# Moving a gate product and a normalisation between engines in a row LSTM, with a new written order

## The chip, the cores and the metric

The kernel runs on one core of one Trainium2 chip. The metric is the device time of a whole execution in microseconds (us). Five engines matter: TensorE (PE, with its weight loads listed apart as PEld), VectorE (DVE), ScalarE (ACT), GpSimd (POOL), and SyncE (SP), which only issues DMAs. Each engine works through its own queue in order, and waits on semaphores that other engines raise.

## The reference, cut to what matters

An image batch of shape (8, 96, 128, 128) is normalised in 32 groups of channels, and then a row LSTM runs down the 128 rows. A row needs the hidden row above it, so rows cannot run side by side.

```python
x_n = gn(x)                                  # (g - mean) / sqrt(var + eps), 32 groups
its = conv(x_n, W_is * mask)                 # width 3, 96 -> 384 channels; the mask leaves
                                             # the left and (by thirds) the centre tap
def step(h, c, row):                         # once for each of 128 rows
    gates = conv(h, W_ss) + row              # width 3, 96 -> 384 channels
    f, i, o = sigmoid(three quarters); g = tanh(the fourth)
    c = f * c + i * g
    h = o * tanh(c)
out = x + h of every row
```

All data are 32-bit floats.

## The kernel before, in words

The batch is cut into two halves of four images (`s` = 0 and 1). A **half-step** `n = 2*row + s` computes one row of one half; there are 256, and the two halves take turns, so that one half's gates are worked on while the other half's products run. Before the first half-step, all of x is read once for the group statistics (some 140 us); that part is not touched.

The pixels of a row are held as even and odd pixels (64 each), and the width-3 convolution is done with fewer products: of the hidden row `hx` the kernel forms a sum `vs` (`total`, letter S), a difference `vf` (`difference`, F), both on VectorE, and two shifted differences `vd` (`shifted`, D), on GpSimd. Of x's 64 "own" channels the like is formed ahead of time into `xs` (letters P, Q, E below); x's 32 "shared" channels are normalised into partitions 96 to 127 of `hx` and ride along with the hidden row.

The 384 gate channels are three PSUM banks A, B, C per half-step, each 128 partitions (sorted so that bank A holds all of f, B all of i, C all of o in partitions 0 to 95, and each a third of g in partitions 96 to 127) by 512 columns (even half, odd half). Every product is 64 rows deep and 256 columns wide; TensorE holds two such products side by side, one in rows 0 to 63 and one in rows 64 to 127 ("lanes" below), and each product is two passes in the trace (two LDWEIGHTS, two MATMULs). A half-step has 33 products: `1`, `2`, `0`, `3` twice for each bank (they use `vs`, `vf`, and both halves of `vd`), and `P`, `Q`, `E` once for each bank. The order between them is:

- `1`, `2`, `P`, `Q` into the bank, then `cp` (`copy`, ScalarE) copies the even half with the bias into an SBUF tile `m`, then `lo` and `hi` (`even`, `odd`, VectorE) replace the two halves by sum and difference, then `0`, `3`, `E` are accumulated on top.
- `si` and `ta` (`sigmoid`, `tanh`, ScalarE) make the gates, `fg` is f*c, `gt` (`gated`) i*g, `ce` (`cell`) the sum, `th` its tanh, `ou` (`output`) o*tanh(c), written into the next row of `hx`. `re` (`residual`) adds h to x in place, on GpSimd, and the result is stored.
- `W` calls `prepare`, the work for the next block of four rows: for one image of the half, `widen` (normalise the own channels), the sum and the two differences into `xs` (all GpSimd), `normalise_shared` for the shared channels (GpSimd), and at times `load_rows` (a DMA).

The scheduler is switched off for PE, ScalarE, VectorE and GpSimd (`manual_schedule`): instructions stand in each engine's queue in the order of the string `PERIOD`, which `do(n, PERIOD)` walks once per half-step. A mark shifts a name to another half-step: `'` is n-1, `''` is n-2, `+` is n+1 (for S, F, D two are added). So one walk of the string holds the products of half-step n, the gates of n-1, and the residual of n-2. A trailing `a` or `b` means the even or the odd pixels alone.

One explicit dependency matters below: `shifted` on GpSimd waits until VectorE has done the last of S and F (`self.last`).

Of the kernel before, what the change touches and what calls it, by code (L numbers as in the profile page):

```python
# [21 lines left out]
def kernel(  # L22
# [35 lines left out]
    NH = 2  # L58
# [232 lines left out]
    def norm(engine, dst, src, lo, layout, b):  # L291
        s, j = divmod(b, BH)
        scale, shift = rstd[s][lo:P, layout, j : j + 1], nmr[s][lo:P, layout, j : j + 1]
        if engine is nc.scalar:
            return engine.activation(dst, src, AF.Identity, bias=shift, scale=scale)  # L295
        else:
            return engine.tensor_scalar(dst, src, scale, shift, ALU.mult, ALU.add)  # L297
# [11 lines left out]
            s * BH + j,  # L309
        )  # L310

    def combine(xw, n, total, differences):

        e, o = xw[:, 0:n, 0:J], xw[:, 0:n, J + 1 :]
        nc.gpsimd.tensor_add(total, e, o)  # L315
        nc.gpsimd.tensor_sub(  # L316
            differences,
            strided(xw[:, 0, :], 0, [(W + 1, n), (J, 2), (1, J)]),
            strided(xw[:, 0, :], J + 1, [(W + 1, n), (0, 2), (1, J)]),
        )  # L320

    def own_image(s, k, j):

# [11 lines left out]
            to[:, r, 1:3, lo:hi].rearrange("p t b j -> p b t j"),  # L335
        )

    normalised = {}

    def normalise_shared(engine, s, k, j, lo, hi):  # L340

        normalised[s, k] = norm(
            engine,
            strided(
                hx[s][k % 2][C:P, lo, 0, j, :],
                0,
                [(2 * BH * JP, hi - lo), (BH * JP + 1, 2), (1, J)],
            ),
            (x0[C:P, 1, j : j + 1] if s == 1 and k == lo == 0 else xt[s, k][C:P, j, lo:hi, :])
            .rearrange("p r (j t) -> p r t j", t=2),  # L350
            C,
            0,
            s * BH + j,
        )
# [53 lines left out]
    class HalfStep:  # L408


        def __init__(self, n):
            self.n, (self.row, self.s) = n, divmod(n, NH)
            self.ps, self.m1, self.moving, self.done, self.gates, self.th = {}, {}, {}, set(), None, None
            self.started, self.images, self.halves, self.writer = set(), {}, {}, {}
            self.hx = hx[self.s][self.row // R % 2][:, self.row % R]
            self.xs = xs[self.s][self.row // R % 2][:, self.row % R]
            self.c = cs[self.s].rearrange("p t b j -> p (t b j)")
# [102 lines left out]
            nc.scalar.activation(self.part(g, lo, hi, t), self.part(ps, lo, hi, t), AF.Tanh)  # L520


        def sigmoid(self, a):
            if self.row == 0 and a == 0:
                return
            gate = self.ps[a][0:C]
            nc.scalar.activation(gate, gate, AF.Sigmoid)  # L527

        def forget(self):
            f = self.ps[0][0:C]  # L530
# [3 lines left out]
        def gated(self, lo=0, hi=BH, t=None):  # L534
            to = self.g if self.row > 0 else self.c
            to, i, g = (self.part(ap, lo, hi, t) for ap in (to, self.ps[1][0:C], self.g))
            nc.vector.tensor_mul(to, i, g)  # L537


        def part(self, ap, lo, hi, t=None):  # L540
            ap = ap.rearrange("p (t b j) -> p t b j", t=2, b=BH)
            return ap[:, :, lo:hi] if t is None else ap[:, t, lo:hi]
# [28 lines left out]
        def total(self, engine=nc.vector, lo=0, hi=BH):  # L571
            e, o = self.pair(lo, hi)
            self.last = engine.tensor_add(self.operand("vs")[:, 0, lo:hi], e, o)  # L573
            row, s = divmod(self.n + 1, NH)
            if engine is nc.vector and row >= R and row % R < 2 and (s, row // R) in normalised:
                tc.add_manual_dep(
                    self.last.ins,
                    normalised[s, row // R].ins.name,
                    mybir.DependencyInfo(mybir.DependencyClass.Sync, mybir.DependencyReason.DATA),
                    reason="the next difference finds the next rows of x normalised",  # L580
                )

        def difference(self, engine=nc.vector, lo=0, hi=BH):
            e, o = self.pair(lo, hi)
# [2 lines left out]
        def shifted(self, lo=0, hi=BH):  # L587
            h = self.hx[:, 0, lo, :]
            diff = nc.gpsimd.tensor_sub(  # L589
                self.operand("vd", 2)[:, :, lo:hi],  # L590
                strided(h, 1, [(BH * JP - 1, 2), (JP, hi - lo), (1, J)]),
                strided(h, 0, [(BH * JP + 1, 2), (JP, hi - lo), (1, J)]),
            )
            if self.last.ins.engine != E.Pool:
                tc.add_manual_dep(
                    diff.ins,
                    self.last.ins.name,
                    mybir.DependencyInfo(
                        mybir.DependencyClass.Sync, mybir.DependencyReason.SCHED_ONLY
                    ),  # L600
                    reason="GpSimd starts when VectorE is done with both SBUF reads",
                )

        def residual(self):
            s, row = self.s, self.row
            xo = xt[s, row // R][0:C, :, row % R, :].rearrange("p b (j t) -> p t b j", t=2)
            (nc.gpsimd if 2 * row + s < last else nc.vector).tensor_add(xo, xo, self.h)  # L607

    def store(s, k, lo, hi):
        nc.sync.dma_start(  # L610
# [6 lines left out]

    SHARED = (((0, 0, R), (3, 0, 1)), ((1, 0, R),), ((2, 0, R),), ((3, 1, R),))

    def own(s, *images):  # L620
        return [(own_image, s, 1, j) for j in images]

    def shared(s, k, *images):
        return [
            (normalise_shared, nc.gpsimd, s, k, *(j if isinstance(j, tuple) else (j, 0, R)))
            for j in images
        ]

    FIRST = [
        own(0, 0),  # L630
        own(0, 1),
        own(0, 2) + shared(0, 1, 0, 1),
        own(0, 3) + [(load_rows, 0, 2)] + shared(0, 1, 2, 3),
        own(1, 0, 1),
        own(1, 2) + shared(1, 1, 0, 1),
        own(1, 3) + [(load_rows, 1, 2)] + shared(1, 1, 2, 3),
        [(own_image, 0, 2, 0), (own_image, 1, 2, 0)],
    ]

    def work(n):  # L640
        if n < len(FIRST):
            return FIRST[n]
        row, s = divmod(n, NH)
        k, r = divmod(row, R)
        parts = []
        if r == R - 1 and k + 2 < NB:
            parts.append((own_image, s, k + 2, 0))
        elif r < R - 1 and k + 1 < NB:
            parts.append((own_image, s, k + 1, r + 1))
        if k + 1 < NB:  # L650
            parts += shared(s, k + 1, *SHARED[r])
        if r == R - 2 and k + 2 < NB:
            parts.append((load_rows, s, k + 2))
        return parts

    worked = set()

    def prepare(n):
        if n not in worked:
            worked.add(n)  # L660
            for part, *args in work(n):
                part(*args)

    def finish(n):
        prepare(n)
# [10 lines left out]


    PERIOD = (
        "2A hiC' siA' D'' 1B 1A taA' 2B fg' 3C' 1A 0C' re'' taB' 2A 2B EC' 1B cpA 0C' 2C W loA cpB "
        "3C' 1C siB' loB PB+ QA+ hiA taCb' 2C hiB taCa' 0A gtb' 1C siC' gta' EA 0B ceb' cpC 3A PA+ "  # L680
        "cea' thb' PC+ 3B loC tha' QC+ oub' EB oua' QB+ 3A F' 3B 0A S' 0B"
    )
    PIXELS = {"a": (0, BH, 0), "b": (0, BH, 1)}
    SPLIT = ("taC", "gt", "ce", "th", "ou")
    PARTS = {
# [12 lines left out]
    def do(n, names, by_lanes=False):  # L698

        for name in names.split():  # L700
            if name == "W":
                prepare(n - 1)
                continue
            at = n
            for mark, offset in (("'", -1), ("+", 1), ("*", 2)):
                at += offset * name.count(mark)
                name = name.replace(mark, "")
            pixels = PIXELS[name[-1]] if name[:-1] in SPLIT and name[-1] in PIXELS else ()
            whole_name = name[:-1] if pixels else name
            tile_ = whole_name[-1] if whole_name[-1] in order else ""  # L710
            part = whole_name[: len(whole_name) - len(tile_)]

            if part in ("S", "F", "D"):
                at += NH
            if not 0 <= at <= last:
                continue
            step = half_step(at)
            if name in step.done or whole_name in step.done:
                continue
            if by_lanes and (part in OWN or part in H_PRODUCTS) and (  # L720
                at < last or part in ("P", "Q") or (part, order[tile_]) in step.halves
            ):
                if step.piece(part, order[tile_]):
                    step.done.add(name)
                continue
            step.done.add(name)
            getattr(step, PARTS[part])(*([order[tile_]] if tile_ else []), *pixels)
            if by_lanes and part == "re":
                finish(at)
# [273 lines left out]
```

## Time and profile before

| what | us |
| --- | --- |
| three runs | 2023.32, 2023.80, 2024.15 (median 2023.8) |
| the profiled execution | 2027.04, its span 2025.2 |
| 153 to 2018 us of the span | the row LSTM; from about 205 us on, one half-step every 7.33 us |
| time before that | statistics of x, and the first rows |
| granted TensorE clock | 0.997 |

The profile is one execution. Its times are taken from its own span; the three unprofiled runs lie about 3 us below it, and a forecast made against the span is moved by the same difference to the median. An instruction's duration and the distance between the starts of two neighbours on an engine are not the same: a short activation's neighbour starts before it has ended, a long one's only after. Where a sum below needs the second, it is read from starts in the timeline.

A few groups (by line, with shapes kept apart) that the later text does not show again:

| group | count | mean us |
| --- | --- | --- |
| GpSimd, own channels: widen 128x512 / sum 128x256 / differences 128x512 | 252 each | 0.816 / 0.641 / 1.070 |
| GpSimd, shared channels 32x512, 32x384, 32x128 | 188, 64, 60 | 0.816, 0.696, 0.464 |
| GpSimd, shifted differences / residual | 255 | 1.041 / 1.297 |
| VectorE, gate product 96x256 | 506 | 0.412 |

### The profile page before, as it was taken

Reading aid. Unit: us, or ns where it says so; the run is one execution under the profiler, and the core shown is the slowest. Engines: PE = TensorE matmul, PEld = TensorE weight load, DVE = VectorE, ACT = ScalarE, POOL = GpSimd, SP = SyncE. Lnnn points to the kernel's source line nnn. Section 1 sums busy time; section 2 is a strip of 40 time slices with the busy share of each in tenths; the row PEclk is TensorE's granted clock in tenths of the full one; section 3 lists DMA queues with packets and bytes.
Section 4 is the critical chain, followed back from the end, with each engine's and each line's share of the span. In section 5 each row is a group of like instructions: output and inputs, shape, how many; then the busy total and the mean of one; then the engine's idle time right before and its main releaser. Section 6 shows DMA issues by size and latency. Waiting matters only on the chain.

```text
span 2025.2 us, 44842 instructions
## 1 busy us (share of the span) xinstructions
PE 1923.3 (95%) x16936; PEld 1831.0 (90%) x16936; DVE 1529.1 (76%) x3996; ACT 1494.9 (74%) x3161; POOL 1473.1 (73%) x1712
## 2 busy tenths in 40 slices
PE   0289999999999999999999999999999999999998
PEld 0178999999999999999999999999999999999997
DVE  5767777777777777777777777777777777777776
ACT  3776777777777777777777777777777777777776
POOL 3348777777777777777777777777777777777752
PEclk9989999999999999999999999999999999999999
DMA  9994333444334334433433443343344333434411
GB/s 374 424 310 100 98 103 91 112 115 104 82 89 113 92 101 115 113 83 82 110 95 95 116 116 95 79 100 96 93 116 116 96 82 96 107 92 106 116 33 32
DMA packets 103382, 237.11 MB, mean 117 GB/s; under 512 B 5952, under 2 KB 8896, under 8 KB 97280
## 3 DMA queue, kind: packets, MB, share of 16 engines
q1 hardware_dynamic: 103168, 234.25, 42.0%
q8 instruction: 135, 2.21, 0.5%
q14 instruction: 79, 0.65, 0.1%
HBM read 183.90 MB, written 50.33 MB: 116 GB/s over the span
## 4 chain that ended last, share of the span: by engine, by line
PE 93%; DMA 4%; ACT 2%; DVE 1%; issue 0%; SPq 0%; POOL 0%; DVEq 0%; POOLq 0%
PE ps L442 92%; DMA piece<-in_x_dram 3%; DMA xs<-in_x_dram 1%; ACT piece L216 1%; PE ps L174 0%; ACT piece L217 0%; DVE bst L876 0%; ACT hx L295 0%; ACT piece L295 0%; DVE hx L560 0%; ACT xs L216 0%; ACT xs L217 0%; SPq L864 0%; PE pv L251 0%; DVE ps L516 0%
## 5 line engine op out<-in xcount | busy, mean ns | idle before, releaser
L442 PE MATMUL ps<-vd,wl 64*128 64x256 f32 (+1 forms) x6096 | 1390.9, 379 | 0.3
L442 PEld LDWEIGHTS ps<-vd,wl 64*128 64x128 f32 (+1 forms) x6096 | 1028.4, 186 | 45.7 <-issue 2.4
L442 PE MATMUL ps<-vs,wm 64*128 64x256 f32 (+1 forms) x3052 | 775.1, 380 | 4.9 <-POOL vs L573 4.4
L442 PE MATMUL ps<-vf,wm 64*128 64x256 f32 (+1 forms) x3052 | 766.3, 377 | 0.0
L527 ACT ACTIVATE ps<-ps 96x512 f32<-96x512 f32 x766 | 441.6, 577 | 356.2 <-PE ps L442 348.1
L442 PE MATMUL ps<-xs,wx 64*128 64x256 f32 x3080 | 637.8, 377 | 11.1 <-POOL xs L315 11.1
L589 POOL TENSOR_TENSOR vd<-hx 128x512 f32<-128x512 f32 x257 | 266.7, 1038 | 388.5 <-PE ps L442 384.8
L442 PEld LDWEIGHTS ps<-xs,wx 64*128 64x128 f32 x3080 | 494.0, 187 | 14.2 <-POOL xs L315 11.6
L520 ACT ACTIVATE g<-ps 32x256 f32<-32x256 f32 (+1 forms) x1021 | 468.6, 482 | 26.7 <-PE ps L442 6.3
L442 PEld LDWEIGHTS ps<-vf,wm 64*128 64x128 f32 (+1 forms) x3052 | 475.4, 187 | 11.0 <-PE ps L442 0.4
L442 PEld LDWEIGHTS ps<-vs,wm 64*128 64x128 f32 (+1 forms) x3052 | 459.6, 186 | 21.6 <-POOL vs L573 5.4
L512 DVE TENSOR_TENSOR ps<-m,ps 128x256 f32<-128x256 f32 x768 | 326.0, 425 | 192.5 <-ACT m L508 182.0
L442 PE MATMUL ps<-xs,wt 64*128 64x256 f32 x1530 | 453.2, 377 | 0.6 <-DVE ps L516 0.6
L508 ACT ACTIVATE m<-ps,wl 128x256 f32<-128x256 f32 x766 | 361.6, 474 | 90.9 <-PE ps L442 84.3
L532 DVE TENSOR_TENSOR ps<-ps,c 96x512 f32<-96x512 f32 x254 | 176.8, 696 | 232.9 <-PE ps L442 226.9
L607 POOL TENSOR_TENSOR x<-x,hx 96x512 f32<-96x512 f32 x255 | 330.8, 1297 | 6.7 <-DVE hx L560 6.7
L516 DVE TENSOR_TENSOR ps<-m,ps 128x256 f32<-128x256 f32 x768 | 300.8, 422 | 1.3 <-PE ps L442 1.2
L442 PEld LDWEIGHTS ps<-xs,wt 64*128 64x128 f32 x1530 | 280.0, 186 | 12.8 <-DVE ps L516 1.0
L316 POOL TENSOR_TENSOR xs<-xw 128x512 f32<-128x512 f32 (+1 forms) x254 | 270.9, 1067 | 0.0
L297 POOL TENSOR_SCALAR hx<-x,rstd,nmr 32x384 f32<-32x384 f32 (+2 forms) x312 | 225.8, 724 | 33.2 <-DMA x<-in_x_dram 1.1
L297 POOL TENSOR_SCALAR xw<-xr,rstd,nmr 128x512 f32<-128x512 f32 x252 | 205.6, 816 | 7.1 <-DVE nmr L289 6.5
L537 DVE TENSOR_TENSOR g<-ps,g 96x256 f32<-96x256 f32 x507 | 189.0, 413 | 3.8 <-ACT g L520 3.8
(91 smaller groups left out, 1223.1 us busy)
## 6 DMA issues: line engine op xcount, KB each, us to landing
xr<-in_x_dram SPq DMA_DIRECT2D x124, 512.0 KB, 6.4
x<-in_x_dram SPq DMA_DIRECT2D x63, 768.0 KB, 6.1
out_dram<-x SPq DMA_DIRECT2D x62, 768.0 KB, 4.6
xs<-in_x_dram SPq DMA_DIRECT2D x30, 1024.0 KB, 12.3
piece<-in_x_dram SPq DMA_DIRECT2D x16, 1024.0 KB, 12.3
x<-in_x_dram SPq DMA_DIRECT2D x62, 256.0 KB, 3.2
xs<-in_x_dram SPq DMA_DIRECT2D x4, 512.0 KB, 8.7
out_dram<-x SPq DMA_DIRECT2D x2, 576.0 KB, 3.7
```

The costliest lines, as they stand in the source:

```text
L297: return engine.tensor_scalar(dst, src, scale, shift, ALU.mult, ALU.add)
L316: nc.gpsimd.tensor_sub(differences, strided(xw[:, 0, :], 0, [(W + 1, n), (J, 2), (1, J)]), strided(xw[:, 0, :], J + 1, [(W + 1, n), (0, 2) ...
L442: made = nc.tensor.matmul(self.ps[a][:, bass.ts(half, HB)][:, cols], weights[rows, bass.ts(a, P)], rhs[rows, cols], start=new, stop=False, ...
L508: nc.scalar.activation(self.m1[a], m1, AF.Identity, bias=column)
L512: nc.vector.tensor_add(self.ps[a][:, 0:HB], self.m1[a], self.ps[a][:, HB:])
L516: nc.vector.tensor_sub(hi, self.m1[a], hi)
L520: nc.scalar.activation(self.part(g, lo, hi, t), self.part(ps, lo, hi, t), AF.Tanh)
L527: nc.scalar.activation(gate, gate, AF.Sigmoid)
L532: nc.vector.tensor_mul(f, f, self.c)
L537: nc.vector.tensor_mul(to, i, g)
L589: diff = nc.gpsimd.tensor_sub(self.operand("vd", 2)[:, :, lo:hi], strided(h, 1, [(BH * JP - 1, 2), (JP, hi - lo), (1, J)]), strided(h, 0, ...
L607: (nc.gpsimd if 2 * row + s < last else nc.vector).tensor_add(xo, xo, self.h)
```

## The change

- The even pixels' part of i*g (`gta`) is done by GpSimd. [...]the sigmoid of bank B is split in two halves of 256 columns (`siBb` in place, `siBa` into a new SBUF tile `i`). From half-step 3 on this holds for all but the last.
- The shared channels are normalised on ScalarE (one image per half-step, 32x512 or 32x384), and the few 32x128 parts on VectorE; both are called `U` and stand for half-step n-2.
- The own channels' work is cut in three (`W1`, `W2`, `W3`: widen, sum, differences), which stand apart in the string; `load_rows` follows the last of them. The first block's work is laid out anew (`FIRST`, `LATER`): one image per half-step, with one image spread over three.
- S stands before F; products of `vs` stand before products of `vf`. The dependency of `total` on the GpSimd normalisation goes. `residual` is, like `shifted`, held until VectorE has done the last of S and F of its half.
- `PERIOD` is rewritten: among others `siA` moves from the start of the next walk to the end of its own, `hiA` stands directly behind `loA`, `taA'` stands between `cpA` and `cpB`, `P+` of banks B and C come first, and `gtb'` stands before `hiB`.

```diff
-    def combine(xw, n, total, differences):
-        e, o = xw[:, 0:n, 0:J], xw[:, 0:n, J + 1 :]
-        nc.gpsimd.tensor_add(total, e, o)
+    def add_pixels(xw, n, total):
+        nc.gpsimd.tensor_add(total, xw[:, 0:n, 0:J], xw[:, 0:n, J + 1 :])
+    def subtract_pixels(xw, n, differences):
         nc.gpsimd.tensor_sub(
...
-        def sigmoid(self, a):
+        def sigmoid(self, a, lo=0, hi=BH, t=None):
             if self.row == 0 and a == 0:
                 return
-            gate = self.ps[a][0:C]
-            nc.scalar.activation(gate, gate, AF.Sigmoid)
+            gate = self.part(self.ps[a][0:C], lo, hi, t)
+            if t == 0 and self.n > NH:
+                self.even_input = self.tile("i", (C, HB))
+                to = self.even_input.rearrange("p (b j) -> p b j", b=BH)
+            else:
+                to = gate
+            nc.scalar.activation(to, gate, AF.Sigmoid)
...
-            nc.vector.tensor_mul(to, i, g)
+            if t == 0 and self.even_input is not None:
+                i = self.even_input.rearrange("p (b j) -> p b j", b=BH)
+                nc.gpsimd.tensor_mul(to, i, g)
+            else:
+                nc.vector.tensor_mul(to, i, g)
...
-            row, s = divmod(self.n + 1, NH)
-            if engine is nc.vector and row >= R and row % R < 2 and (s, row // R) in normalised:
-                tc.add_manual_dep(
...
-            (nc.gpsimd if 2 * row + s < last else nc.vector).tensor_add(xo, xo, self.h)
+            made = (nc.gpsimd if 2 * row + s < last else nc.vector).tensor_add(xo, xo, self.h)
+            following = steps.get(self.n + NH)
+            if self.n < last and following is not None:
+                following.hold(made)
...
-    def own(s, *images):
-        return [(own_image, s, 1, j) for j in images]
+    def own(s, k, j, buffer=0):
+        to, wide = xs[s][k % 2], xw[buffer]
+        return (
+            (widen, nc.gpsimd, wide, 0, R, s, k, j, 0),
+            (add_pixels, wide, R, to[:, :, 0, j, :]),
+            (subtract_pixels, wide, R, to[:, :, 1:3, j, :]),
+        )
     def shared(s, k, *images):
+        parts = [j if isinstance(j, tuple) else (j, 0, R) for j in images]
         return [
-            (normalise_shared, nc.gpsimd, s, k, *(j if isinstance(j, tuple) else (j, 0, R)))
-            for j in images
+            (normalise_shared, nc.vector if hi == 1 else nc.scalar, s, k, j, lo, hi)
+            for j, lo, hi in parts
         ]
+    spread = own(1, 1, 0, 1)
     FIRST = [
-        own(0, 0),
-        own(0, 1),
-        own(0, 2) + shared(0, 1, 0, 1),
-        own(0, 3) + [(load_rows, 0, 2)] + shared(0, 1, 2, 3),
-        own(1, 0, 1),
-        own(1, 2) + shared(1, 1, 0, 1),
-        own(1, 3) + [(load_rows, 1, 2)] + shared(1, 1, 2, 3),
-        [(own_image, 0, 2, 0), (own_image, 1, 2, 0)],
+        ([], own(0, 1, 0), []),
+        (shared(0, 1, 0, 1), own(0, 1, 1), []),
+        (shared(0, 1, 2, 3), own(0, 1, 2), []),
+        (shared(1, 1, 0, 1), own(0, 1, 3), [spread[0], (load_rows, 0, 2)]),
+        (shared(1, 1, 2), own(1, 1, 1), [spread[1]]),
+        (shared(1, 1, 3), own(1, 1, 2), [spread[2]]),
+        ([], own(1, 1, 3), [(load_rows, 1, 2)]),
+        ([], own(0, 2, 0), []),
     ]
+    LATER = dict(zip((9, 11, 13), own(1, 2, 0, 1)))
...
     PERIOD = (
-        "2A hiC' siA' D'' 1B 1A taA' 2B fg' 3C' 1A 0C' re'' taB' 2A 2B EC' 1B cpA 0C' 2C W loA cpB "
-        "3C' 1C siB' loB PB+ QA+ hiA taCb' 2C hiB taCa' 0A gtb' 1C siC' gta' EA 0B ceb' cpC 3A PA+ "
-        "cea' thb' PC+ 3B loC tha' QC+ oub' EB oua' QB+ 3A F' 3B 0A S' 0B"
+        "1A hiC' D'' U 1B fg' 2A 2B siBb' 0C' 1A re'' taB' 3C' 2A 1B siBa' EC' 2B cpA 3C' W1 1C "
+        "taA' loA 0C' 2C cpB hiA PB+ PC+ W2 taCb' loB 2C taCa' 0A gtb' 1C gta' siC' 3A hiB PA+ "
+        "ceb' QB+ cpC W3 3B cea' EA thb' loC 0B tha' QC+ oub' 3A oua' EB 0A S' 0B QA+ F' siA 3B"
     )
-    SPLIT = ("taC", "gt", "ce", "th", "ou")
+    SPLIT = ("taC", "siB", "gt", "ce", "th", "ou")
...
-            if name == "W":
-                prepare(n - 1)
+            if name[0] == "U":
+                if n >= NH:
+                    prepare(n - NH, "U")
+                continue
+            if name[0] == "W":
+                prepare(n - 1 + name.count("+") - name.count("'"), name.strip("W+'"))
                 continue
```

More of the change, by code (lines that the diff above doesn't have):

```diff
@@ L320, in combine @@
         )
+    def combine(xw, n, total, differences):
+        add_pixels(xw, n, total)
+        subtract_pixels(xw, n, differences)
     def own_image(s, k, j):
@@ L336, in own_row @@
         )
-    normalised = {}
     def normalise_shared(engine, s, k, j, lo, hi):
-        normalised[s, k] = norm(
+        norm(
             engine,
@@ L414, in __init__ @@
             self.started, self.images, self.halves, self.writer = set(), {}, {}, {}
+            self.even_input = self.last = None
             self.hx = hx[self.s][self.row // R % 2][:, self.row % R]
@@ L573, in total @@
             self.last = engine.tensor_add(self.operand("vs")[:, 0, lo:hi], e, o)
-            row, s = divmod(self.n + 1, NH)
-            if engine is nc.vector and row >= R and row % R < 2 and (s, row // R) in normalised:
-                tc.add_manual_dep(
[L577 to L581, printed above, removed]
         def difference(self, engine=nc.vector, lo=0, hi=BH):
@@ L593, in shifted, with hold @@
             )
-            if self.last.ins.engine != E.Pool:
+            self.hold(diff)
+        def hold(self, made):
+            if self.last is not None and self.last.ins.engine != E.Pool:
                 tc.add_manual_dep(
-                    diff.ins,
+                    made.ins,
                     self.last.ins.name,
@@ L644, in work, with prepare @@
         k, r = divmod(row, R)
[L645 to L662, printed above, removed]
+        ahead, image = (k + 2, 0) if r == R - 1 else (k + 1, r + 1)
+        return (
+            shared(s, k + 1, *SHARED[r]) if k + 1 < NB else [],
+            own(s, ahead, image) if ahead < NB else (),
+            ([(load_rows, s, k + 2)] if r == R - 2 and k + 2 < NB else [])
+            + ([LATER[n]] if n in LATER else []),
+        )
+    worked = {}
+    def prepare(n, which="123"):
+        scalar, image, rest = worked.setdefault(n, [list(parts) for parts in work(n)])
+        now = []
+        if "U" in which:
+            now, scalar[:] = list(scalar), []
+        for i in "123":
+            if i in which and int(i) <= len(image) and image[int(i) - 1]:
+                now.append(image[int(i) - 1])
+                image[int(i) - 1] = None
+        if image.count(None) == len(image) and n not in closed:
+            closed.add(n)
+            now += rest
+        for part, *args in now:
+            part(*args)
+    closed = set()
     def finish(n):
```

## The prediction

> **What bounds the kernel now.** I read the page first, then the timeline of one half-step engine by engine, then the form-separated list for ScalarE. From the page, the busy line and the chain:
>
> ```profile
> PE 1923.3 (95%) x16936; PEld 1831.0 (90%) x16936; DVE 1529.1 (76%) x3996; ACT 1494.9 (74%) x3161; POOL 1473.1 (73%) x1712
> PE 93%; DMA 4%; ACT 2%; DVE 1%; issue 0%; SPq 0%; POOL 0%; DVEq 0%; POOLq 0%
> ```
>
> TensorE bounds it; the other three are a quarter idle. "Busy" does not say that both lanes run, though. The timeline of the weight loads shows one lane standing still once in each half-step:
>
> ```profile
> 1004.55 0.19 PEld L442 LDWEIGHTS ps<-vd,wl 64*128 64x128 f32 x1
> 1004.59 0.19 PEld L442 LDWEIGHTS ps<-vs,wm 64*128 64x128 f32 x1
> 1004.77 0.44 PEld L442 LDWEIGHTS ps<-xs,wx 64*128 64x128 f32 x4
> 1005.24 0.36 PEld L442 LDWEIGHTS ps<-vf,wm 64*128 64x128 f32 x2
> 1005.74 0.18 PEld L442 LDWEIGHTS ps<-vd,wl 64*128 64x128 f32 x1
> 1005.77 0.18 PEld L442 LDWEIGHTS ps<-vs,wm 64*128 64x128 f32 x1
> ```
>
> On each lane a pass follows the last after 0.216 us (1004.55 to 1004.77), so a product takes 0.433 and 33 of them on two lanes 33 x 0.433 / 2 = 7.13 us. From 1005.24 on only `2C` is loaded; `0A` (the `vd` load), due on the other lane at about 1005.2, comes at 1005.74. The timelines of VectorE and ScalarE tell what it waited for:
>
> ```profile
> 1004.39 0.90 DVE L512 TENSOR_TENSOR ps<-m,ps 128x256 f32<-128x256 f32 x2 [0.70 <-ACT m L508]
> 1005.20 0.76 DVE L516 TENSOR_TENSOR ps<-m,ps 128x256 f32<-128x256 f32 x2
> ...
> 1001.76 0.57 ACT L527 ACTIVATE ps<-ps 96x512 f32<-96x512 f32 x1 [1.38 <-PE ps L442]
> 1002.37 1.21 ACT L520 ACTIVATE g<-ps 32x512 f32<-32x512 f32 x2
> 1003.89 0.94 ACT L508 ACTIVATE m<-ps,wl 128x256 f32<-128x256 f32 x2 [0.31 <-PE ps L442]
> 1004.73 0.58 ACT L527 ACTIVATE ps<-ps 96x512 f32<-96x512 f32 x1
> 1005.33 0.65 ACT L520 ACTIVATE g<-ps 32x256 f32<-32x256 f32 x2
> 1006.01 0.57 ACT L527 ACTIVATE ps<-ps 96x512 f32<-96x512 f32 x1
> 1006.61 0.47 ACT L508 ACTIVATE m<-ps,wl 128x256 f32<-128x256 f32 x1
> 1006.99 0.73 ACT L552 ACTIVATE th<-c 96x256 f32<-96x256 f32 x2
> ```
>
> `hiA` (the first of the two at 1005.20, 0.42 long) ends at 1005.62 and `0A` loads 0.12 later. `hiA` stood behind `loB`, which waited for `cpB`, which waited for the second `1B`. That is a loop, and it gives the period: `1B` (two passes to its end, 0.59, and 0.04 to ScalarE) + `cpB` 0.475 + 0.03 + `loB` to `hiA` 0.335 + `hiA` 0.42 + 0.22 to `0A` at full cadence + 0.04 for the other lane behind it + 12 products on that lane to the next `1B`, 5.18 = 7.33. The timeline has `siA` at 1001.76 and again at 1009.10: 7.33 to 7.34. So 0.20 us of a half-step is lost, some 50 us in the whole run, and nothing else is to be had.
>
> **What the Trainium skill says.** "ScalarE: Activation LUTs", What ACT_TABLE_LOAD costs: an activation costs 186 ns plus 0.833 ns an element, 93 more for each pointer operand, and neighbours overlap by 93 ns. The trace agrees on durations (`th`, 256 wide: 0.411; 399 ns by the page) but on the overlap only for 256 columns: `cpC` to `th` is 0.38 for 0.47, yet behind 512 columns the next starts 0.02 after the end (1006.01 + 0.57, then 1006.61). "SBUF — State Buffer", Who interferes with whom: VectorE with two SBUF inputs contends with GpSimd reading SBUF. Only S and F have two; in the trace of before they run at 1000.97 to 1001.73, where GpSimd idles, so that cost isn't seen. "GPSIMD Engine Reference", 3.1 Elementwise, has GpSimd's tensor_tensor at about twice VectorE's time; here 0.641 (128x256 add) against 0.42.
>
> **The change, part by part.**
>
> GpSimd loses 188, 64 and 60 normalisations: 153.3 + 44.6 + 27.9 = 226 us, 0.9 a half-step, and gains a product of 96x256. Not shown in this form; between 0.641 (the sum of the same width) and 1.3 (the residual, strided, twice as wide). I take 0.65. GpSimd ends at 5.7 of 7.3 us: no bound.
>
> VectorE loses one of its two gate products (0.335 of its queue) and gains 60 small normalisations (about 0.35 each). No bound.
>
> ScalarE is what matters. It gains 188 normalisations 32x512 and 64 of 32x384, and `siB` becomes two halves. The price of the first is in the profile, since the first rows already use it:
>
> ```profile
> L295 ACT ACTIVATE hx<-x,nmr,rstd 32x512 f32<-32x512 f32 x4 | 3.4, 839 | 0.1
> L295 ACT ACTIVATE piece<-xr,nmr,rstd 128x384 f32<-128x384 f32 x4 | 3.0, 738 | 0.1
> ```
>
> It has 0.84, not the 0.6 of a 512-column sigmoid. The split of `siB` costs about 0.08 more than the whole. ScalarE rises from about 5.6 to 6.5 us of 7.3, and, more to the point, the new work stands at the head of its queue: `siA U siBb taB siBa cpA taA cpB`. Nothing there can overtake.
>
> The stall of before goes: `hiA` now follows `loA` at once. With `cpA` free, `0A` would come in time. But what is late next? `3B` (place 23 of the 33 products) waits for `hiB`, which stands behind `loB` and `gtb`; `loB` waits for `cpB`, which now stands behind everything above. And the head, `siA`, waits for the last `0A` of the walk (place 29), three products behind `3B` on the same lane. That closes a loop of one half-step:
>
> - place 29 to its end 0.59, to ScalarE 0.04
> - `siA` 0.60 (1001.76 to 1002.37)
> - `U` 0.84 + 0.02 = 0.86
> - `siBb` 0.36 (0.577 less the 0.22 by which tanh 32x512 exceeds 32x256, 0.592 against 0.369) + 0.03, as `taB` waits for it
> - `taB` 0.61 (half of 1.21, and the gap)
> - `siBa` 0.29 (second of the two 256-wide tanh: 0.65 - 0.37)
> - `cpA` 0.37 (`cpC` to `th`), `taA` 0.61, `cpB` 0.475 + 0.03
> - `loB` to `gtb` to `hiB` 2 x 0.335, `hiB` 0.42
> - `hiB` to `3B` 0.155 (F ended at 1001.39; its product's loads began 0.05 later and the product some 0.1 after those)
> - `3B` to place 29: three products, 1.30
>
> Sum 7.41. In every fourth row `U` has 384 columns: 0.738 less an overlap of 0.10 instead of 0.86, so 7.19. Mean 7.36. The two lanes wait for each other where they share a bank (`3A` behind `EA`, `EB` behind `0B`), and after a stall on one lane the other runs behind; I add 0.03 for it, an estimate. So 7.39 against 7.33: 0.06 x some 246 half-steps = +14 us.
>
> The rest costs nothing while that loop holds. S before F, and `vs` products first: S ends about 7.4 after `siA`, the next `1A` needs it about 0.3 later. `gta` on GpSimd: starts at `taCa`'s end, 4.8 after `siA`, when D, `re`, W1 and W2 (1.0 + 1.28 + 0.89 + 0.62) have been done for some 0.4; `cea` then comes at 5.5 instead of 5.2 and `tha`, `oua`, S behind it. That cover is the same 0.3; if it goes, S is late and each further 0.1 costs about 0.05 a half-step (the loop through S spans two). W3 (1.07) ends 0.4 ahead of S. The hold on `residual` names an instruction that D, ahead of it, has already waited for: nothing. The dropped dependency of `total` was not waited for: VectorE has no such wait between half-steps. `load_rows` behind W3: SP's two DMAs wait for W1's read of `xr` either way, and the data (6.4 us to landing) are wanted two half-steps on. `U` for n-2 comes a half-step later than `W` had it, after the same load: more slack. The early `P` products of B and C take banks freed in the half-step before; those of A wait for `gtb`, at place 21, a little before it.
>
> First half-steps: in before, seven of them take 5.7 us more than 7 x 7.33, behind GpSimd. GpSimd gets less there, ScalarE two `U` in three half-steps (3 x 0.86). Nothing net, within 3 us.
>
> Profiled execution: 2027 + 14 = 2041; against the median of 2023.8, which lies 3 below, **2038**.
>
> **The rivals.**
>
> *ScalarE is not late (faster).* If 512-wide activations overlapped their neighbours by the page's 93 ns, `siA`, `U`, `taB`, `taA` would give back 4 x 0.115 = 0.46, the loop would be 6.9 to 7.0, and the next bound that of S, about 7.2: 0.11 to 0.13 x 246, 1995. For it: ScalarE idles 1.4 us before `siA` now. Against: no 512-wide instruction in this trace overlaps. It decides from 0.06 off the 3.75 us between `siA` and `cpB`; at just that it is no change, 2024.
>
> *No change.* The two loops come out alike within 4 us; my sum is not that sharp.
>
> *GpSimd's product is the late link (much slower).* At 1.3 instead of 0.65, or pushed onto S by W3, S comes 0.65 later: (7.41 + 7.41 + 0.3) / 2 to 7.54, +50 us, 2075. For it: the residual's rate. Against: contiguous operands, and 0.641 for the like.
>
> *The product of `siB` and GpSimd isn't used.* No: each walk has it from half-step 3 on.
>
> **How the numbers follow.** Forecast (2028 to 2055) 0.56, much slower 0.16, no change 0.08, faster 0.20. A difference under 0.2% (4 us) is about what a measurement of this kernel cannot tell from none. The bounds of the loop's unknowns (`siBb` and the waits each 0.03, `U` 0.75 to 0.87, the lanes 0 to 0.1) make 7.27 to 7.49, 2009 to 2063; extended to most of the faster and half the much slower case: 1998 to 2068. Slower 0.72, same 0.08, faster 0.20.
>
> **What would show it.** ScalarE's starts from `siA` to `cpB` 3.75 apart (`U` 0.84 in place), the wait of ScalarE before `siA` shrunk to about 0.9; the idle spell of the weight loads not before `0A` of place 18 but before `3B` of place 23, released by `hiB`; half-steps of 7.4, one pair of four shorter. I am wrong if `siA` to `cpB` is under 3.6, or if the lane stands before `1A` (S) instead.

## The result, and the profile after

The changed kernel takes 2156.4 us (median of 4 runs, 2156.0 to 2157.2) against 2023.6 for the kernel before beside it: ratio 1.066, 95% interval 1.064 to 1.068. It is slower, as forecast, but by 133 us where the forecast had 14, and it lies far above the range. The granted clock is 0.998 (0.997 before), and the span of the profiled execution is 2154.2 us.

From the page of the changed kernel, the busy line and the chain:

```profile
PE 2046.6 (95%) x16936; PEld 1869.0 (87%) x16936; DVE 1571.0 (73%) x3804; ACT 1736.5 (81%) x3662; POOL 1429.5 (66%) x1656
PE 84%; DVE 6%; ACT 5%; DMA 4%; issue 1%; POOL 0%; SPq 0%; POOLq 0%; DVEq 0%
```

TensorE still reads 95% busy, with the same 16936 matmuls. The weight loads tell more: 87% instead of 90%. And on the chain PE has 84% where it had 93%; most of the difference went to VectorE and ScalarE. So TensorE waits for them.

A half-step, taken from its first `th` to the first `th` of the next, was 7.33 to 7.34 throughout. Of eight half-steps now, the two that hold a 32x128 normalisation take 8.08, the one after them 7.90, the others with 32x512 7.84, and the two with 32x384 7.72; the mean is 7.88. 0.54 x 246 half-steps = 133 us: all of the difference lies there.

ScalarE's timeline of one such half-step of the changed kernel (start, duration, then the instruction; in brackets the idle time before it and who ended it), from `siA` to `taC`:

```profile
1003.45 0.57 ACT L538 ACTIVATE ps<-ps 96x512 f32<-96x512 f32 x1 [1.05 <-PE ps L448]
1004.05 0.85 ACT L295 ACTIVATE hx<-x,nmr,rstd 32x512 f32<-32x512 f32 x1
1004.80 0.36 ACT L538 ACTIVATE ps<-ps 96x256 f32<-96x256 f32 x1
1005.25 0.59 ACT L526 ACTIVATE g<-ps 32x512 f32<-32x512 f32 x1
1005.86 0.38 ACT L538 ACTIVATE i<-ps 96x256 f32<-96x256 f32 x1
1006.26 0.47 ACT L514 ACTIVATE m<-ps,wl 128x256 f32<-128x256 f32 x1
1006.76 0.59 ACT L526 ACTIVATE g<-ps 32x512 f32<-32x512 f32 x1
1007.38 0.47 ACT L514 ACTIVATE m<-ps,wl 128x256 f32<-128x256 f32 x1
1007.88 0.65 ACT L526 ACTIVATE g<-ps 32x256 f32<-32x256 f32 x2
```

From `siA` to `cpB` it never waits for another engine: a queue that runs through, 3.93 us from start to start. VectorE behind it, `loB`, `gtb`, `hiB`:

```profile
1007.89 0.43 DVE L518 TENSOR_TENSOR ps<-m,ps 128x256 f32<-128x256 f32 x1 [0.22 <-ACT m L514]
1008.29 0.42 DVE L552 TENSOR_TENSOR g<-ps,g 96x256 f32<-96x256 f32 x1
1008.63 0.41 DVE L522 TENSOR_TENSOR ps<-m,ps 128x256 f32<-128x256 f32 x1
```

And the weight loads there:

```profile
1007.82 0.18 PEld L448 LDWEIGHTS ps<-vs,wm 64*128 64x128 f32 x1
1007.89 0.19 PEld L448 LDWEIGHTS ps<-vd,wl 64*128 64x128 f32 x1
1007.95 0.19 PEld L448 LDWEIGHTS ps<-vs,wm 64*128 64x128 f32 x1
1008.10 0.40 PEld L448 LDWEIGHTS ps<-vd,wl 64*128 64x128 f32 x2
1008.82 0.33 PEld L448 LDWEIGHTS ps<-xs,wx 64*128 64x128 f32 x4 [0.32 <-PE ps L448]
```

Now both lanes stand still, for 0.32 us, before a product of `xs`: `PA+` at place 21, which goes into the bank that `gtb` reads last. The view names PE as the releaser, but the last product into that bank belongs to the walk before and ended almost 5 us earlier. What came last is `gtb`: it ended at 1008.71, and the loads follow 0.11 later.

### The profile page after: what moved, and what is told of

Read it like the earlier page. It is cut to its first block, busy times and chain, and to the rows that moved or that the text cites. A ratio compares the mean times of both kernels' runs of the same rounds, so it can differ in the third digit from the quotient of the medians.

```text
span 2154.2 us, 45180 instructions
## 1 busy us (share of the span) xinstructions
PE 2046.6 (95%) x16936; PEld 1869.0 (87%) x16936; DVE 1571.0 (73%) x3804; ACT 1736.5 (81%) x3662; POOL 1429.5 (66%) x1656
## 4 chain that ended last, share of the span: by engine, by line
PE 84%; DVE 6%; ACT 5%; DMA 4%; issue 1%; POOL 0%; SPq 0%; POOLq 0%; DVEq 0%
PE ps L448 83%; DMA xs<-in_x_dram 4%; DVE hx L297 2%; ACT m L514 1%; ACT hx L295 1%; DVE g L552 1%; DVE ps L518 1%; DVE ps L543 1%; ACT g L526 1%; DVE bst L911 1%; ACT ps L538 1%; ACT xs L216 0%; ACT xs L217 0%; POOL xw L297 0%; POOL xs L314 0%
## 5 line engine op out<-in xcount | busy, mean ns | idle before, releaser
L448 PE MATMUL ps<-vd,wl 64*128 64x256 f32 (+1 forms) x6096 | 1471.5, 379 | 1.0 <-DVE ps L522 0.6
L448 PEld LDWEIGHTS ps<-vd,wl 64*128 64x128 f32 (+1 forms) x6096 | 1094.6, 186 | 48.2 <-POOL xs L314 12.9
L448 PE MATMUL ps<-vs,wm 64*128 64x256 f32 (+1 forms) x3052 | 833.2, 380 | 4.1 <-POOL vs L588 3.9
L448 PE MATMUL ps<-vf,wm 64*128 64x256 f32 (+1 forms) x3052 | 823.0, 377 | 0.1
L538 ACT ACTIVATE ps<-ps 96x256 f32<-96x256 f32 (+1 forms) x767 | 385.0, 502 | 277.4 <-PE ps L448 269.2
L448 PEld LDWEIGHTS ps<-vs,wm 64*128 64x128 f32 (+1 forms) x3052 | 515.6, 187 | 15.9 <-POOL vs L588 5.0
L448 PEld LDWEIGHTS ps<-xs,wx 64*128 64x128 f32 x3080 | 405.0, 187 | 105.8 <-PE ps L448 91.8
L550 POOL TENSOR_TENSOR g<-i,g 96x256 f32<-96x256 f32 x252 | 182.4, 724 | 254.2 <-ACT g L526 254.2
L522 DVE TENSOR_TENSOR ps<-m,ps 128x256 f32<-128x256 f32 x768 | 323.7, 422 | 10.0 <-PE ps L448 1.2
L295 ACT ACTIVATE hx<-x,nmr,rstd 32x512 f32<-32x512 f32 (+1 forms) x255 | 208.7, 818 | 6.7
L562 DVE TENSOR_TENSOR c<-ps,g 96x256 f32<-96x256 f32 x508 | 205.5, 417 | 0.5
```

What stands on the lines that cost most here:

```text
L448: made = nc.tensor.matmul(self.ps[a][:, bass.ts(half, HB)][:, cols], weights[rows, bass.ts(a, P)], rhs[rows, cols], start=new, stop=False, ...
L522: nc.vector.tensor_sub(hi, self.m1[a], hi)
L538: nc.scalar.activation(to, gate, AF.Sigmoid)
L562: nc.vector.tensor_add(c, f, g)
```

## The experiments

All start from the changed kernel unless said otherwise. Times are medians; the runs of one kernel agree within 5 us, mostly 2. Ratios are to the kernel before, on the same chip (2023.8 to 2024.4 us).

The theory: the loop that the prediction wrote down is real (`siA` through ScalarE's queue to `cpB`, VectorE, a product, `siA` again), but its gate is `PA+` behind `gtb`, not `3B` behind `hiB`, and its ScalarE part is longer than was added up. The rivals: S (fed by GpSimd's slow product) is late; or the 32x128 parts are.

**e1_pa_late: the gate.**

```diff
-        "taA' loA 0C' 2C cpB hiA PB+ PC+ W2 taCb' loB 2C taCa' 0A gtb' 1C gta' siC' 3A hiB PA+ "
-        "ceb' QB+ cpC W3 3B cea' EA thb' loC 0B tha' QC+ oub' 3A oua' EB 0A S' 0B QA+ F' siA 3B"
+        "taA' loA 0C' 2C cpB hiA PB+ PC+ W2 taCb' loB 2C taCa' 0A gtb' 1C gta' siC' 3A hiB QC+ "
+        "ceb' QB+ cpC W3 3B cea' EA thb' loC 0B tha' PA+ oub' 3A oua' EB 0A S' 0B QA+ F' siA 3B"
```

> Base is the changed kernel (2156 us, 7.84 us a half-step in the middle). Only `PA+` (place 21 of the 33 products) and `QC+` (place 26) trade places. Main theory, the loop from siA through ScalarE's queue to cpB, loB, gtb and then `PA+`, which waits for gtb to free its bank: that gate goes, and the next one in the same loop, `3B` (place 23) behind hiB, is 0.16 us earlier in the half-step. Half-step 7.84 -> about 7.68, some -39 us, about 2117 us; the lane then stands before `3B`. Rival, the lane's stall at place 21 is only where the lateness of S or of GpSimd's product shows up: no change, 2156 within 6 us.

2126.6 us, ratio 1.051 (1.050 to 1.053), so 30 us less; 7.68 a half-step, as expected. The rows with 32x128 stayed at 8.09, which is the missing quarter of the 39. In its weight loads the stall has moved to `3B`, released by `hiB` (VectorE's L522):

```profile
1002.84 0.61 PEld L448 LDWEIGHTS ps<-xs,wx 64*128 64x128 f32 x4
1003.61 0.18 PEld L448 LDWEIGHTS ps<-vd,wl 64*128 64x128 f32 x1 [0.16 <-DVE ps L522]
```

This is the stall that the prediction had announced. It comes out only once `PA+` is out of the way.

**e2_u_late: what the normalisation costs where it stands.**

```diff
-        "1A hiC' D'' U 1B fg' 2A 2B siBb' 0C' 1A re'' taB' 3C' 2A 1B siBa' EC' 2B cpA 3C' W1 1C "
+        "1A hiC' D'' 1B fg' 2A 2B siBb' 0C' 1A re'' taB' 3C' 2A 1B siBa' EC' 2B cpA 3C' W1 1C "
...
-        "ceb' QB+ cpC W3 3B cea' EA thb' loC 0B tha' QC+ oub' 3A oua' EB 0A S' 0B QA+ F' siA 3B"
+        "ceb' QB+ cpC W3 3B cea' EA thb' loC 0B tha' QC+ oub' 3A oua' EB 0A S' 0B QA+ F' U siA 3B"
```

> Base is the changed kernel. Only `U` (the shared channels' normalisation on ScalarE, the small ones on VectorE) moves, from between siA and siBb to the end of the walk ahead of siA, where ScalarE is idle for 1.05 us. Main theory, U is paid in the loop siA -> cpB -> loB -> gtb -> PA+ : 0.76 us leave the loop (0.852 less what the neighbours then lose), which would be 7.08; another bound then takes over, between the 7.13 us of TensorE's products and 7.25. Half-step about 7.2, total about 2000 us (1985 to 2015), faster than the kernel before. Rival, the bound is S or GpSimd's gate product rather than ScalarE's head: less than 20 us gained, 2136 to 2156.

2069.4 us, ratio 1.022 (1.021 to 1.024): 87 us less by moving one letter. `U` also stands for VectorE's 32x128 parts, but the half-steps that have none fell as well, by 0.2 to 0.3, so it is the head of ScalarE's queue that counts. A half-step is 7.50, though, not 7.2. The next loop came sooner than thought. In ScalarE's timeline of this run, `siBa`, `cpA`, `taA`, `cpB`:

```profile
1005.73 0.38 ACT L538 ACTIVATE i<-ps 96x256 f32<-96x256 f32 x1
1006.40 0.47 ACT L514 ACTIVATE m<-ps,wl 128x256 f32<-128x256 f32 x1 [0.29 <-PE ps L448]
1006.90 0.59 ACT L526 ACTIVATE g<-ps 32x512 f32<-32x512 f32 x1
1007.52 0.47 ACT L514 ACTIVATE m<-ps,wl 128x256 f32<-128x256 f32 x1
```

`cpA` now waits for TensorE, and then `taA` stands between it and `cpB`, with `gtb` and `PA+` behind.

**e3_v_pool: the rows of 8.08.**

```diff
-            (normalise_shared, nc.vector if hi == 1 else nc.scalar, s, k, j, lo, hi)
+            (normalise_shared, nc.gpsimd if hi == 1 else nc.scalar, s, k, j, lo, hi)
```

> Base is the changed kernel. Only the 32x128 normalisations (two in eight half-steps) go from VectorE to GpSimd. Main theory, on VectorE each stands behind GpSimd's residual for about 1 us (1.32 us long instead of about 0.3) and makes fg and the gates after it late: these half-steps go from 8.08 to about 7.84, some 60 x 0.25 = -15 us, about 2141 us. Rival, the longer half-steps come from something else of these rows (the loads or another order in GpSimd's queue): no change, or slower by up to 60 x 0.46 = 28 us if GpSimd then is late.

2142.0 us, ratio 1.058 (1.057 to 1.060): 14 us less, and those rows at 7.84 to 7.86. In the changed kernel VectorE has, in such a row, the 32x128 part and `fg` behind it:

```profile
1028.21 1.32 DVE L297 TENSOR_SCALAR hx<-x,rstd,nmr 32x128 f32<-32x128 f32 x1 [0.86 <-ACT hx L295]
1029.56 0.70 DVE L543 TENSOR_TENSOR ps<-ps,c 96x512 f32<-96x512 f32 x1
```

and GpSimd its residual:

```profile
1028.14 1.30 POOL L617 TENSOR_TENSOR x<-x,hx 96x512 f32<-96x512 f32 x1
```

The small part first waits 0.86 for ScalarE's `U` on the same rows of `hx`. Then it begins 0.06 after the residual and ends 0.09 after it, 1.32 us for work that takes 0.35 in e2_u_late, where it stands away from the residual:

```profile
1004.18 0.35 DVE L297 TENSOR_SCALAR hx<-x,rstd,nmr 32x128 f32<-32x128 f32 x1
```

`taA` then waits for `fg`, 0.28 on ScalarE, and from this the 0.24 of these rows comes. The Trainium skill, "SBUF — State Buffer", Who interferes with whom, says that VectorE and GpSimd share a pair of ports, that whoever has it first blocks the other for a whole instruction, and names `tensor_scalar` among the operations that can take it. The trace agrees, with 1.32 beside the residual against 0.35 away from it.

**e4_gate_dve and e12_gate_psum: is GpSimd's product late?** The first takes gta back to VectorE with the tile `i` kept, the second goes all the way back to PSUM.

```diff
-                nc.gpsimd.tensor_mul(to, i, g)
+                nc.vector.tensor_mul(to, i, g)
```

```diff
-            if t == 0 and self.n > NH:
+            if False:
```

> Base is the changed kernel. Only the even pixels' product gta goes back from GpSimd to VectorE, still out of the SBUF tile i. Main theory, GpSimd's product is not the late link and VectorE's queue was helped by its leaving: no gain; hiB and what follows stand up to 0.33 us later or not, according to where gta stands (behind gtb, ahead of hiB), so slower by 0 to 0.18 us a half-step, 2156 to 2200 us. Rival, the product on GpSimd (0.72 instead of about 0.35) makes the cell, its tanh and S late: faster by 0.1 to 0.3 us a half-step, 2080 to 2130 us.

> The changed kernel with gta on VectorE as in the kernel before (siBa in place, no tile i), so without the meeting of two SBUF operands and GpSimd that slowed some of e4_gate_dve's products (0.52 us on average instead of 0.41). Main theory, GpSimd's product is not the late link in the changed kernel: hiB and `3B` come 0.335 later than in e1_pa_late's loop (7.68), 8.0 to 8.05 a half-step, 2190 to 2220 us. Rival, the product on GpSimd (0.72) is what makes the changed kernel late: 2060 to 2130 us.

2226.0 us, ratio 1.100 (1.098 to 1.101), and 2228.2 us, 1.101 (1.099 to 1.102). Both are some 70 us slower than the changed kernel, more than either text allowed. The rival falls: in this order the product is better on GpSimd, although it takes longer there. In e4_gate_dve both gates open late, `PA+` and then `3B`:

```profile
1007.16 0.33 PEld L448 LDWEIGHTS ps<-xs,wx 64*128 64x128 f32 x4 [0.52 <-PE ps L448]
1007.77 0.18 PEld L448 LDWEIGHTS ps<-vd,wl 64*128 64x128 f32 x1 [0.28 <-DVE ps L522]
```

**e5_u_late_pa_late: both moves of e1 and e2.**

> e2_u_late (2069 us, 7.50 us a half-step) with `PA+` and `QC+` also exchanged. In e2_u_late two loops are nearly alike: (a) second `2A` -> cpA -> taA -> cpB -> loB -> gtb -> `PA+`, 7.5, and (b) first `1A` -> second `2A` -> cpA -> taA -> cpB -> taC -> gta on GpSimd -> cea, tha, oua -> S -> `1A`, read as 7.48 (1003.94 to 1011.42). If (b) is real, freeing `PA+` alone brings nearly nothing: 7.48, 2060 to 2069 us. Rival, S has slack and only `PA+` holds: as in e1_pa_late 0.16 less, 7.34, about 2030 us.

2040.0 us, ratio 1.008 (1.006 to 1.009), 7.37: between the two. The loop through S exists: S ends at 1005.21, and the loads of the first `1A` follow 0.05 later.

```profile
1004.79 0.42 DVE L588 TENSOR_TENSOR vs<-hx 128x256 f32<-128x256 f32 x1
1005.27 0.37 PEld L448 LDWEIGHTS ps<-vs,wm 64*128 64x128 f32 x3
```

But it is 7.37 long, not 7.48: in e2_u_late S had ended 0.13 before `1A` loaded, and that slack had been counted into the loop.

**e6_ta_before_cp, e7_ta_before_cp_pa_late_v_pool, e8_ta_first: another order of the same ScalarE work.** e6 is e2 with `taA` before `cpA` and `siBa` after it:

```diff
-        "1A hiC' D'' 1B fg' 2A 2B siBb' 0C' 1A re'' taB' 3C' 2A 1B siBa' EC' 2B cpA 3C' W1 1C "
-        "taA' loA 0C' 2C cpB hiA PB+ PC+ W2 taCb' loB 2C taCa' 0A gtb' 1C gta' siC' 3A hiB PA+ "
+        "1A hiC' D'' 1B fg' 2A 2B siBb' 0C' 1A re'' taB' 3C' 2A 1B taA' EC' 2B cpA 3C' W1 1C "
+        "siBa' loA 0C' 2C cpB hiA PB+ PC+ W2 taCb' loB 2C taCa' 0A gtb' 1C gta' siC' 3A hiB PA+ "
```

e7 adds the edits of e1 and e3. e8 is e7 with `siA taA siBb taB siBa cpA cpB` instead (`taA'` written behind `D''`, ahead of `fg'`).

> e2_u_late with taA moved ahead of cpA (into ScalarE's wait before cpA) and siBa behind cpA; nothing else. Then only siBa (0.40) stands between cpA and cpB instead of taA (0.62): cpB 0.21 earlier, and with it both loops (a) through `PA+` and (b) through S. Half-step 7.50 -> about 7.29, about 2018 us (2008 to 2030), level with or just below the kernel before. Rival, another order of the same ScalarE work changes nothing because TensorE's own waits (`0C`, `EC`) set the rest: 2060 to 2070.

> e6_ta_before_cp with `PA+` and `QC+` exchanged and the 32x128 normalisations on GpSimd, which idles there. Loop (b) through S stays at about 7.27; the rows with 32x128 parts lose another 0.06. About 2010 us (2000 to 2025). Rival, with U late and V away the lane wait at `PA+` was the only one left: 7.15, below 1990.

> U late, `PA+` and `QC+` exchanged, 32x128 parts on GpSimd, and taA at the head: ScalarE's order is siA taA siBb taB siBa cpA cpB taC, so that taA uses the wait before siBb and nothing stands between cpA and cpB. cpA then comes some 0.14 later, cpB some 0.44 earlier than in e2_u_late (it then waits for the second `2B`). Loop (b) through S falls to about 7.05, so TensorE's 7.13 or the loop through hiA and `0A` (place 18), about 7.2, takes over: 7.15 to 7.25 a half-step, 1985 to 2008 us, faster than both kernels. Rival, ScalarE, busy 6.9 of 7.2 us, can't keep this up and fg behind taA makes the cell late: 7.3 or more, 2020 and above.

e6: 2009.6 us, ratio 0.993 (0.991 to 0.994). e7: **2001.7 us, ratio 0.989 (0.987 to 0.991)**, about 1% faster than the kernel before. The shortest half-steps are 7.23 in both, half of them in e6 and three quarters in e7; the 8 us between the two are the rows with 32x128, 7.37 in e6 and 7.23 in e7. In e7 ScalarE, from `taB` and `taA` together to `taC`:

```profile
1004.31 1.21 ACT L526 ACTIVATE g<-ps 32x512 f32<-32x512 f32 x2
1005.58 0.47 ACT L514 ACTIVATE m<-ps,wl 128x256 f32<-128x256 f32 x1
1005.96 0.37 ACT L538 ACTIVATE i<-ps 96x256 f32<-96x256 f32 x1
1006.22 0.47 ACT L514 ACTIVATE m<-ps,wl 128x256 f32<-128x256 f32 x1
1006.94 0.65 ACT L526 ACTIVATE g<-ps 32x256 f32<-32x256 f32 x2 [0.25 <-PE ps L448]
```

`cpA` and `cpB` start 0.64 apart, where it was 1.12 in the changed kernel, because `siBa` now stands between them, with 0.26 to the next start, where `taA` took 0.62. And `taA` has gone ahead of `cpA`, into time in which ScalarE had waited for TensorE (0.29 in e2_u_late).

e8 missed its forecast, and the number fell in its rival's range: 2042.6 us, ratio 1.009 (1.008 to 1.011), 7.41. All gates of n-1 but `taC` and `siC` now stand before `cpA`: `siA` to `cpA` is 2.68 (6.11 to 8.79 us after 1000) instead of e7's 2.48, without a wait for another engine longer than 0.03, and `loA`, `hiA`, `0A` hang on it. It looks like the prediction's mistake in another place, a head of queue priced one wait at a time; that is not shown, as no run took it apart.

**e9_0a_later: what bounds e7.** `QC+` and `QB+` take the places before `0A` and `3A`.

```diff
-        "siBa' loA 0C' 2C cpB hiA PB+ PC+ W2 taCb' loB 2C taCa' 0A gtb' 1C gta' siC' 3A hiB QC+ "
-        "ceb' QB+ cpC W3 3B cea' EA thb' loC 0B tha' PA+ oub' 3A oua' EB 0A S' 0B QA+ F' U siA 3B"
+        "siBa' loA 0C' 2C cpB hiA PB+ PC+ W2 taCb' loB 2C taCa' QC+ gtb' 1C gta' siC' 0A hiB QB+ "
+        "ceb' 3A cpC W3 3B cea' EA thb' loC 0B tha' PA+ oub' 3A oua' EB 0A S' 0B QA+ F' U siA 3B"
```

> e7_ta_before_cp_pa_late_v_pool (2002 us, 7.23 us a half-step) with `QC+` and `QB+` brought forward, so that `0A` stands at place 20 instead of 18 and `3A` at 22. In e7 `0A` starts 0.12 after hiA and 0.13 late on its lane; if that loop (second `2A` -> cpA -> loA -> hiA -> `0A`, the one of the kernel before) still bounds it, 0.05 to 0.1 goes, until the loop through S (7.16) takes over: 7.15 to 7.18, 1985 to 1992 us. Rival, the loop through S and the lanes' waits for each other (second `1A` behind `2A`, `EC` behind `3C`, 0.1 each) already hold: no change, 1999 to 2005.

1999.5 us, ratio 0.988 (0.986 to 0.990): not told from e7, and again 7.23 in the middle. The rival holds in that `0A` isn't the bound. Which of the rest makes 7.23 of 7.13 stays open.

**e10_best_gate_dve and e11_best_gate_psum: the product on GpSimd, in the good order.** These are e7 with the edits of e4 and e12.

> e7_ta_before_cp_pa_late_v_pool with gta back on VectorE (out of the SBUF tile i). If moving the product was sound and only its written order was at fault, this is slower: hiB, ceb, cea and S stand 0.33 later in VectorE's queue, less the 0.3 by which VectorE's product is shorter than GpSimd's for cea: 0.1 to 0.3 a half-step, 2025 to 2075 us. Rival, the product on GpSimd (0.72) is a burden in this order too: no change or faster, 1985 to 2002.

> e7_ta_before_cp_pa_late_v_pool with gta on VectorE as in the kernel before: siBa in place in PSUM, no tile i, gta reads one operand from PSUM and one from SBUF. In e10_best_gate_dve gta took 1.09 us where it met GpSimd's differences (1002.61 to 1003.70; GpSimd 1002.36 to 1003.42), 0.41 where it did not, and the half-steps without a meeting took 7.36. Main theory, two SBUF operands and GpSimd at work is what made e10 slow: here gta takes 0.41 throughout and a half-step 7.36, about 2030 us. Rival, VectorE's order (hiB behind gta) is what costs: as e10, 2150 to 2165 us.

e10: 2161.8 us, ratio 1.068 (1.066 to 1.069). That is 160 us above e7, where 23 to 73 were expected. VectorE's gtb and gta there:

```profile
1002.27 0.42 DVE L552 TENSOR_TENSOR g<-ps,g 96x256 f32<-96x256 f32 x1
1002.61 1.09 DVE L550 TENSOR_TENSOR g<-i,g 96x256 f32<-96x256 f32 x1
```

and GpSimd:

```profile
1002.36 1.06 POOL L318 TENSOR_TENSOR xs<-xw 128x512 f32<-128x512 f32 x1
```

Two products of one shape, 0.42 and 1.09; the slow one has both operands in SBUF and runs while GpSimd reads SBUF, until 0.28 after GpSimd is done. The same page of the skill states this case also (two SBUF inputs against a GpSimd instruction that reads). In e11, with one operand in PSUM, the group of all gate products is

```profile
L552 DVE TENSOR_TENSOR g<-ps,g 96x256 f32<-96x256 f32 x326 | 122.4, 415 | 1.5
```

0.415 on average, and the kernel takes 2032.9 us, ratio 1.0045 (1.003 to 1.006), 7.35 in most half-steps, where 2030 was expected. So in a good order the product on GpSimd is worth 31 us (e7 against e11), and 129 more would have been lost by leaving it on VectorE with both operands in SBUF.

## Why the prediction was wrong

In us of a mean half-step (the kernel before: 7.335), from the forecast to the measured 7.876:

| step | half-step | what shows it |
| --- | --- | --- |
| forecast | 7.39 | |
| terms mis-sized | 7.66 | e1_pa_late, rows with 32x128 taken at its 7.68 |
| gate taken to be `3B` | 7.81 | e3_v_pool |
| 32x128 "no bound" | 7.876 | the changed kernel |

- **The loop** was right, and with it the direction: `siA`, ScalarE's queue, `cpB`, VectorE, a product, back to `siA`. Moving `U` out of it gave 87 us at once (e2). The rival that ScalarE is not late falls, and so does "no change".
- **The gate was the step of the mechanism that failed**, worth 0.15. The prediction wrote that the `P` products of A "wait for `gtb`, at place 21, a little before it", and then let the loop close through `3B` at place 23 behind `hiB`. It never compared the two. `gtb` ends 0.335 before `hiB`, but place 21 is two products, 0.43, earlier, and the load comes 0.11 behind the end instead of 0.05: `PA+` is the tighter by 0.16. e1 took just that away.
- **The terms were mis-sized**, by 0.27, the larger part. `siA` to `cpB` was put at 3.73 by its terms (3.75 among the signs) and is 3.934. `U` to `siBb` is 0.76, less than the 0.86 assumed, because `siBb` does start before `U` ends. But `siBb` to `taB` is 0.45 (0.39 assumed), `siBa` to `cpA` 0.41 (0.29), `cpA` to `taA` 0.50 (0.37): the overlaps read at `cpC` to `th` and between the two 256-wide tanh were carried to pairs that don't have them. The same at `cpB` to `taC` (0.50) made `gtb` and `hiB` about 0.07 later than `loB` alone would. The rest of the loop, from `hiB`'s end over `3B` to `siA`, was 2.085 forecast and is 2.08.
- **The small parts on VectorE** were priced at 0.35 and no bound. They are 0.35 of work, but 1.26 on average behind the residual, with `fg` and `taA` behind them. The prediction had used the skill's page on SBUF for instructions with two SBUF inputs and passed over its line on `tensor_scalar`. That is 0.064 on average, 15 us (14 by e3).
- **GpSimd** was right: its product, 0.72 instead of the 0.65 taken, is not the late link, and GpSimd mostly waits 0.8 to 1.2 us for `taC` before it (e4, e12: 70 us worse without). From the changed kernel:

```profile
1008.60 0.72 POOL L550 TENSOR_TENSOR g<-i,g 96x256 f32<-96x256 f32 x1 [0.92 <-ACT g L526]
```

- **S** had less cover than forecast. It was to end 7.4 after `siA`, with 0.3 to spare; in the half-step shown above it ends 7.79 after, and `1A` loads 0.07 later. At 7.84 that held nobody up; at e5's 7.37 it did.
- **What disappears** was right in part. `hiA` behind `loA` did shorten that wait, but `0A` is still late, since `cpA` is.
- **The split of `siB`** was to cost about 0.08. Its halves take 0.45 and 0.41 of the queue where a whole sigmoid takes 0.60, so it cost 0.25, and most of the 0.27 above is this.
- **The first half-steps** moved nothing of note; the first 14 after the first `th` lost 2.8 us against the steady pace, 4.7 in the kernel before.
- **The signs.** ScalarE's wait before `siA` did shrink, from 1.38 to 1.05 (0.9 was forecast), and one pair of four is shorter. The two signs of being wrong did not come: they looked for a shorter queue and for S, not for a longer queue or another gate on the same one.
- **Three of its figures** come out otherwise, without weight in the result: 33 x 0.433 / 2 is 7.14, the loop through S with GpSimd's product late is 7.56, and 5.7 us is GpSimd's busy time in a half-step of the kernel before (5.5 after the change).

The range was too narrow because it was made of the terms of one loop. A gate left out of the comparison isn't a spread of those terms. And the spread itself, 0.03 for a wait, was too small: the mis-sized terms alone, 0.27 x 246 = 66 us, lead out of the range.

## What to carry to other kernels

When a new order closes a loop, list every product that waits on the queue in question, each with its place and the end it waits for, and take the largest of (end minus place x cadence); the one that comes to mind first needn't be it. Work that nobody waits for does most harm at the head of an in-order queue: the same ScalarE instructions gave 2156 us and, with `U` and `taA` put into its idle spells, 2010 (e6). Move an operand from PSUM to SBUF only after looking at what GpSimd does at that moment.

## What the runs showed of the hardware

- VectorE's product of two SBUF operands took 1.09 us beside GpSimd's SBUF read, 0.41 without it; a 32x128 `tensor_scalar` 1.32 against 0.35. When VectorE came first, as in e2_u_late, GpSimd paid instead, little: 1.14 against 1.04 for the shifted differences.
- ScalarE's neighbours overlap by about 0.1 in some pairs and not at all in others of the same shapes: `siBa` before `cpB` in e7 (0.37 long, the next starts 0.26 later) does, `siBa` before `cpA` in the changed kernel (0.38 long, the next 0.41 later) does not. Nor does length decide it, as was assumed above: behind `U`, 32x512 and 0.85 long, `siBb` starts 0.76 later. Of two pairs on one bank, `siBb` then `taB` stood 0.09 apart in the changed kernel, `siA` then `taA` 0.03 in the kernel before. What decides it wasn't tried.
- When `PA+` waited in the changed kernel, both lanes stopped, for 0.32. The two passes that each lane then loads, the first from 1008.82 on, stand 0.11 apart instead of 0.216, so that some 0.1 of a stall is regained.
